# Additive attention: half of the softmax exponentials as powers of e on GpSimd, in eight pieces each

## The chip, the cores and the metric

The kernel runs on one core of a Trainium2 chip. The metric is device time in microseconds (us) of one execution; lower is better. A core has five engines, each with a queue of its own that it works off strictly in order: PE (TensorE, matrix products), DVE (VectorE), ACT (ScalarE, table functions such as tanh and exp), POOL (GpSimd) and SP (SyncE, which issues transfers). Engines wait for one another through semaphores, so an instruction that waits holds up everything behind it in its own queue.

## The reference, cut to what matters

The network has four layers over x of shape (2, 256, 32, 32). The change lies in the attention of the last layer, which runs over B = 2 images of L = 1024 tokens with D = 256 channels and U = 32 hidden units:

```python
q = jnp.einsum('bld,du->blu', inputs, Wt)
k = jnp.einsum('bld,du->blu', inputs, Wx)
h = jnp.tanh(q[:, :, None, :] + k[:, None, :, :] + bh)
e = jnp.einsum('biju,u->bij', h, Wa[:, 0]) + ba[0]
a = jax.nn.softmax(e, axis=-1)
v = jnp.einsum('bij,bjd->bid', a, inputs)
```

In front of it in the program stands a mixture of experts (top 2 of 8, with gelu), behind it another one. For every pair of tokens there are 32 tanh, 67 million in all, and one exponential, 2 million in all.

## The kernel before, in words

**Tiles and groups.** The 2048 queries are cut into NT = 16 tiles of 128, eight for each image. A tile is worked in M = 8 groups, 128 groups in all; a group is a tile `th` of 128 x 4 x 1024 elements (4 queries x 32 units on the partitions, 4 sets of queries, 1024 keys). For group n:

- `add(n)` (L1336): four DVE instructions of 128x1024 add the query to all keys and write `th`, which has three buffers.
- `tangents(n)` (L1346): one ACT instruction of 128x4096 takes tanh in place. For the 34 "light" groups in the middle (n from 50 to 83) ACT adds one of the four sets itself (L1343, L1344), and DVE has three.
- `score(n)` (L1355): sixteen PE matmul passes sum over the units with the weights Wa into the PSUM tile `ps_e`, 128x1024, of which there is one buffer; eight groups fill it.

**Softmax and values of tile i**, in group n = 8(i+1), when its eight groups are scored: `additive_softmax` (L1408) takes exp of `ps_e` on ACT into `p`, summing each row on the way; L1409 takes the reciprocal of the sum on DVE. Two groups later `turn` transposes the first half of `p` on PE and DVE copies it out (L1368, L1369), one group later the second half, and one more group later `values` multiplies with the tokens (L1376, L1380), and `done` takes the statistics of the finished tile for the next norm.

**Order of the work.** One Python loop runs over n and calls, for each n, `add(n + 2)`, `tangents(n)`, the softmax of the tile that has just ended, `score(n)`, then turns or values; so adds are issued two groups ahead of the tanh. Around each n the caller also steps other work on the same engines: up to n = 61 the rest of the experts before (`second`, one step every two groups) and the projections for the second image (`then`), afterwards the routing of the last layer and its first experts (`first`, one step every four groups). An expert's step has products on PE (L1175, L1189, L1205), their copies on DVE (L1163, L1183, L1211), gelu on ACT (L1192), weights fetched by SP, and two indirect transfers issued by POOL (L1146 gathers the tokens of a block, L1212 scatters its results). A scheduler of the framework decides at build time how the instructions of these strands stand in each engine's queue; in the running kernel the queues are fixed.

**Tables.** ACT's functions come from sets of tables; the instruction ACT_TABLE_LOAD changes the set. In the profile it stands before an exp that follows a gelu (L1408) and before a gelu that follows an exp (L1192); tanh never has one before it.

Of the kernel before, what the change touches and what calls it, by code (L numbers as in the profile page):

```python
# [8 lines left out]

# [1 line left out]

# [11 lines left out]
F32 = mybir.dt.float32  # L25
# [3 lines left out]
AF = mybir.ActivationFunctionType  # L29
ALU = mybir.AluOpType  # L30
AX = mybir.AxisListType
PSUM = bass.MemoryType.PSUM

P = 128
B, C, N = 2, 256, 1024
T = B * N
NT = T // P
CC = C // P
CH = 512
# [48 lines left out]
class Stack:  # L88
# [757 lines left out]
    def tables(self):  # L846

        nc = self.nc
        tl = lambda name, shape, dtype=F32: self.const.tile(shape, dtype, name=f"dp_{name}")
        ctx = ExitStack()  # L850
        tmp = ctx.enter_context(self.tc.tile_pool(name="dp_tmp", bufs=1))
        iota = lambda t, pattern, base, by: nc.gpsimd.iota(
            t, pattern=pattern, base=base, channel_multiplier=by, allow_small_or_imprecise_dtypes=True
        )
        self.iota_lo = tl("lo", [P, P], BF16)
        iota(self.iota_lo, [[1, P]], 0, 0)
        self.iota_hi = tl("hi", [P, BOTH], BF16)
        iota(self.iota_hi, [[1, BOTH]], 0, 0)
        self.iota_block = tl("block", [1, BOTH])
        iota(self.iota_block, [[1, BOTH]], 0, 0)  # L860
        self.partition = tl("partition", [P, 1])
        iota(self.partition, [[0, 1]], 0, 1)


        self.spare = tl("spare", [P, BOTH])
        iota(self.spare, [[P, BOTH]], P + 2 * T, 1)
        self.number = tl("number", [P, B, 2, N // P], BF16)
        iota(self.number, [[2 * N // P, B], [N // P, 2], [1, N // P]], 1, 0)

        before = tmp.tile([P, P], F32, name="dp_before")  # L870
        nc.gpsimd.memset(before, 1.0)
        nc.gpsimd.affine_select(
            before, before, pattern=[[1, P]], compare_op=ALU.is_gt, fill=0.0, base=0, channel_multiplier=-1
        )
        self.before = tl("before_bf", [P, P], BF16)
        nc.vector.tensor_copy(self.before, before)

        W = N // P * E
        d = tmp.tile([W, W + E], I32, name="dp_d")
        iota(d, [[1, W + E]], 0, -1)  # L880
        low = tmp.tile([W, W + E], I32, name="dp_low")
        nc.vector.tensor_scalar(low, d, E - 1, None, ALU.bitwise_and)
        same = tmp.tile([W, W + E], F32, name="dp_same")
        nc.vector.tensor_scalar(same, low, 0.0, None, ALU.is_equal)
        later = tmp.tile([W, W + E], F32, name="dp_later")
        nc.vector.tensor_scalar(later, d, 0.0, None, ALU.is_gt)
        self.earlier = tl("earlier", [W, W + E], BF16)
        nc.vector.tensor_tensor(self.earlier, same, later, ALU.mult)
        self.ones_bf = tl("ones", [P, P], BF16)
        nc.vector.memset(self.ones_bf, 1.0)  # L890
        ctx.close()
# [425 lines left out]
    def additive_attention(self, ctx, aa, t, u, light, done):  # L1317


        tc, nc = self.tc, self.nc  # L1320
        U, R, J, M = self.UNITS, self.ROWS, self.GROUPS, self.FOURS
        sb = ctx.enter_context(tc.tile_pool(name="aa_sb", bufs=1))
        p_e, p_t = (ctx.enter_context(tc.tile_pool(name=f"aa_{n}", bufs=1, space=PSUM)) for n in "et")
        groups = [(i, m) for i in range(NT) for m in range(M)]
        summed, scored = {}, {}

        def keys_and_queries(n, j):
            i, m = groups[n]
            b = i // (N // P)
            return aa["kT"][:, b * N : (b + 1) * N], aa["qb"][:, i, j * M + m : j * M + m + 1]  # L1330

        def add(n):

            h = sb.tile([P, J, N], F32, name="th", bufs=3)
            for j in range(1 if light(n) else 0, J):
                nc.vector.tensor_scalar(h[:, j, :], *keys_and_queries(n, j), None, ALU.add)  # L1336
            summed[n] = h

        def tangents(n):
            h = summed[n]  # L1340
            if light(n):
                keys, query = keys_and_queries(n, 0)
                nc.scalar.activation(h[:, 0, :], keys, AF.Tanh, bias=query)  # L1343
                nc.scalar.activation(h[:, 1:, :], h[:, 1:, :], AF.Tanh)  # L1344
            else:
                nc.scalar.activation(h, h, AF.Tanh)  # L1346

        def score(n):
            i, m = groups[n]
            if m == 0:  # L1350
                scored[i] = p_e.tile([P, 2, CH], F32, name="ps_e")
            h = summed.pop(n)
            for a in range(2):
                for j in range(J):
                    nc.tensor.matmul(  # L1355
                        scored[i][U * j : U * (j + 1), a, :], lhsT=aa["pick"][:, m, :],
                        rhs=h[:, j, a * CH : (a + 1) * CH], start=(m == 0), stop=(m == M - 1),
                    )

        turned = {}  # L1360

        def turn(i, p, a):

            if a == 0:
                turned[i] = sb.tile([P, N // P, P], F32, name="ptT")
            pt = p_t.tile([P, 4, P], F32, name="ps_pt")
            for j in range(4):
                nc.tensor.transpose(pt[:, j, :], p[:, (4 * a + j) * P : (4 * a + j + 1) * P], self.ident)  # L1368
            nc.vector.tensor_copy(turned[i][:, 4 * a : 4 * a + 4, :], pt)  # L1369

        def values(i, rec):
            b = i // (N // P)
            ptT = turned.pop(i)
            av = p_t.tile([P, 4, P], F32, name="ps_pt").rearrange("p k q -> p (k q)")[:, 0:C]
            for j in range(N // P):
                nc.tensor.matmul(  # L1376
                    av, lhsT=ptT[:, j, :], rhs=u[:, b * (N // P) + j, :],
                    start=(j == 0), stop=(j == N // P - 1),
                )
            nc.vector.scalar_tensor_tensor(t[:, i, :], av, rec, t[:, i, :], ALU.mult, ALU.add)  # L1380


        soft = {}
        add(0)
        add(1)
        for n in range(len(groups) + 5):
            if n + 2 < len(groups):
                add(n + 2)
            if n < len(groups):
                tangents(n)  # L1390
            i, m = n // M - 1, n % M
            if i >= 0 and m == 0:
                soft[i] = self.additive_softmax(aa, sb, scored.pop(i))
            if n < len(groups):
                score(n)
            if i >= 0 and m in (2, 3):
                turn(i, soft[i][0], m - 2)
            if i >= 0 and m == 4:
                values(i, soft.pop(i)[1])
                done(i)  # L1400
            yield n

    def additive_softmax(self, aa, sb, pe):

        nc = self.nc
        s, rec = (self.small.tile([P, 1], F32, name=f"aa_{n}") for n in ("s", "rec"))
        p = sb.tile([P, N], F32, name="p")
        nc.scalar.activation(p, pe.rearrange("p a b -> p (a b)"), AF.Exp, bias=aa["ba"], accum_out=s)  # L1408
        nc.vector.reciprocal(rec, s)  # L1409
        return p, rec  # L1410

# [287 lines left out]
class General(Stack):  # L1699
# [446 lines left out]
                    scores(i + 1)  # L2146
                values(i)

    def additive_softmax(self, aa, sb, pe):
        nc = self.nc  # L2150
        m, nb, s, rec = (self.small.tile([P, 1], F32, name=f"aa_{n}") for n in ("m", "nb", "s", "rec"))
        nc.vector.tensor_reduce(m, pe, AX.XY, ALU.max)

        nc.vector.tensor_tensor(m, m, aa["ba"], ALU.add)
        nc.vector.scalar_tensor_tensor(nb, m, -1.0, aa["ba"], ALU.mult, ALU.add)
        p = sb.tile([P, N], F32, name="p")
        nc.scalar.activation(p, pe.rearrange("p a b -> p (a b)"), AF.Exp, bias=nb, accum_out=s)
        nc.vector.reciprocal(rec, s)
        return p, rec
# [98 lines left out]
```

## Time and profile before

| | us |
|---|---|
| median of three runs | 2495.07 (2486.7 to 2497.26) |
| the profiled execution | 2487.81 |
| its span in the profile | 2486.0 |
| additive attention, by the tanh in it | about 1737 to 2295 |
| ACT busy between 1740 and 1950, of 210.00 | 202.53 |
| ACT busy between 1950 and 2100, of 150.00 | 141.11 |
| ACT busy between 2100 and 2300, of 200.00 | 183.94 |
| DVE busy in the same three stretches | 168.94, 118.54, 153.40 |
| POOL busy in the same three stretches | 20.05, 7.06, 28.51 |

The profile is of one execution. Its time is 1.8 us above its span, and 7.3 us under the median. "Busy" is the time in which an engine works on an instruction; of PE it overstates, since matmuls are pipelined. A group's row gives line, engine, operation, output and inputs with shapes, the number of instructions, the busy time, the mean of one in ns, and the idle time before them with what ended it. A timeline's row gives the start, the duration, and in brackets the idle time of the engine before it with its cause.

### The profile page before, as it was taken

The page shows a single profiled execution, that of the slowest core. Times are in us where ns is not written, and L with a number is a line of the kernel's source. Part 1 is how long each engine was busy: PE and PEld are TensorE (multiplying, and loading weights), DVE is VectorE, ACT ScalarE, POOL GpSimd, SP SyncE. Part 2 cuts the span into 40 slices and gives each one's busy share as a digit, 9 for nine tenths or more (in the row PEclk, how much of TensorE's full clock was granted, in tenths as well). Part 3 has the DMA queues.
Part 4 walks back from the last instruction along what each step waited for, and adds up shares of the span by engine and source line. Part 5 has one row for each costly group of instructions (what it writes and reads, how often), then busy time and mean ns, then how long its engine had stood idle before and what let it go on. Part 6 is the DMA issues. An engine that isn't in the chain of part 4 may idle for free.

```text
span 2486.0 us, 42312 instructions
## 1 busy us (share of the span) xinstructions
PE 2337.5 (94%) x17179; PEld 1017.8 (41%) x17179; DVE 1710.7 (69%) x2656; ACT 1398.4 (56%) x1445; POOL 238.4 (10%) x253
## 2 busy tenths in 40 slices
PE   7999999999999999999998969998999888988987
PEld 4333333333333333333333646665444433333654
DVE  5677777785677777876679566226887778876533
ACT  1565556555555556554444333221999999998122
POOL 0000000000000000000002212221110001111332
PEclk9999999999999999999999979999999999999998
DMA  4000000000000000000000036777444103323986
GB/s 140 1 1 1 1 1 1 1 5 1 1 1 1 1 1 1 6 1 1 1 1 10 2 120 252 291 291 269 185 157 187 60 9 104 107 89 110 335 324 232
DMA packets 65121, 205.46 MB, mean 83 GB/s; under 512 B 15060, under 2 KB 29908, under 8 KB 54932
## 3 DMA queue, kind: packets, MB, share of 16 engines
q1 hardware_dynamic: 51428, 176.81, 19.7%
q0 software_dynamic: 8160, 22.29, 2.5%
q10 hardware_dynamic: 5328, 3.55, 0.5%
q8 instruction: 137, 2.24, 0.4%
q14 instruction: 68, 0.56, 0.1%
HBM read 183.09 MB, written 17.44 MB: 81 GB/s over the span
## 4 chain that ended last, share of the span: by engine, by line
PE 72%; DVE 13%; issue 6%; DMA 5%; ACT 3%; POOL 1%; SPq 0%; ACTq 0%; DVEq 0%; POOLq 0%
PE ps_o L237 20%; PE ps_t L215 20%; PE ps_e L1355 7%; PE bk_y L1205 4%; PE bk_h L1175 4%; DVE th L1336 4%; DMA w<-in_l_w 3%; PE ps_row L460 2%; DVE sum L227 2%; PE ps_pt L1376 2%; PE ps_qk L569 1%; PE ps_row L450 1%; PE ps_row L489 1%; PE bk_t L1189 1%; DVE den L263 1%
## 5 line engine op out<-in xcount | busy, mean ns | idle before, releaser
L218 ACT ACTIVATE e<-ps_t 128x1024 f32<-128x1024 f32 x640 | 652.2, 1023 | 481.8 <-PE ps_t L216 470.6
L227 DVE TENSOR_TENSOR sum<-sum,e 128x1024 f32<-128x1024 f32 x592 | 726.2, 1227 | 280.2 <-ACT e L218 268.8
L237 PE MATMUL ps_o<-e,v 64*64 64x512 f32 x5120 | 663.4, 590 | 11.0 <-DVE o L244 7.2
L215 PE MATMUL ps_t<-q,k 64*64 64x512 f32 x2048 | 528.0, 590 | 0.5 <-DVE v L610 0.5
L216 PE MATMUL ps_t<-q,k 64*64 64x512 f32 x2048 | 527.9, 590 | 0.0
L1336 DVE TENSOR_SCALAR th<-kT,qb 128x1024 f32<-128x1024 f32 x478 | 330.6, 750 | 88.0 <-PE ps_e L1355 85.7
L1346 ACT ACTIVATE th<-th 128x4096 f32<-128x4096 f32 x94 | 335.7, 3616 | 16.8 <-DVE th L1336 16.5
L237 PEld LDWEIGHTS ps_o<-e,v 64*64 64x64 f32 x5120 | 191.1, 131 | 371.2 <-issue 178.6
L1355 PE MATMUL ps_e<-th,pick 128*32 128x512 f32 x2048 | 264.3, 613 | 17.7 <-ACT p L1408 9.4
L215 PEld LDWEIGHTS ps_t<-q,k 64*64 64x64 f32 x2048 | 148.0, 133 | 287.4 <-issue 153.0
L1175 PE MATMUL bk_h<-w,xgT 128*128 128x512 f32 x496 | 244.3, 610 | 13.6 <-DVE xgT L1163 7.4
L1205 PE MATMUL bk_y<-w,h 128*128 128x256 f32 x992 | 246.5, 385 | 5.9 <-DVE y L1211 3.2
L1205 PEld LDWEIGHTS bk_y<-w,h 128*128 128x128 f32 x992 | 178.7, 191 | 49.0 <-issue 21.3
L1197 ACT ACTIVATE h<-bk_t,w 128x128 f32<-128x128 f32 x276 | 78.7, 368 | 211.9 <-issue 115.8
L265 POOL TENSOR_TENSOR inverses<-inverses,den 128x512 f32<-128x512 f32 x24 | 30.4, 1268 | 1319.3 <-DVE den L263 1319.3
L216 PEld LDWEIGHTS ps_t<-q,k 64*64 64x64 f32 x2048 | 148.0, 133 | 0.0
L1175 PEld LDWEIGHTS bk_h<-w,xgT 128*128 128x128 f32 x496 | 87.1, 194 | 93.9 <-issue 66.4
L1212 POOL DMA_INDIRECT given<-y,gives x85 | 85.9, 1011 | 400.3 <-DVE y L1211 337.2
L1355 PEld LDWEIGHTS ps_e<-th,pick 128*32 128x32 f32 x2048 | 58.1, 111 | 160.1 <-issue 124.4
L1181 DVE COPY hp<-bk_h 128x512 f32<-128x512 f32 x69 | 47.6, 691 | 106.1 <-PE bk_h L1175 106.1
L1146 POOL DMA_INDIRECT xg<-rows,takes x85 | 86.5, 1017 | 325.6 <-PE bk_x L1158 275.2
L215 PE MATMUL ps_t<-qh,kh 64*64 64x512 f32 x384 | 98.7, 598 | 0.0
(344 smaller groups left out, 2194.3 us busy)
## 6 DMA issues: line engine op xcount, KB each, us to landing
w<-in_l_w SPq DMA_DIRECT2D x39, 1152.0 KB, 5.4
w<-in_l_w SPq DMA_DIRECT2D x39, 1030.0 KB, 7.3
w<-in_l_w SPq DMA_DIRECT2D x46, 640.0 KB, 6.8
w<-in_l_w SPq DMA_DIRECT2D x46, 514.0 KB, 5.8
b<-in_l_w SPq DMA_DIRECT2D x16, 512.0 KB, 8.3
b<-in_l_w SPq DMA_DIRECT2D x23, 256.0 KB, 5.4
rows<-u SPq DMA_DIRECT2D x8, 512.0 KB, 2.9
uT<-given SPq DMA_DIRECT2D x32, 128.0 KB, 3.2
```

Source lines behind the costliest of these rows:

```text
L215: nc.tensor.matmul(ps[part, 0, :], lhsT=ka[:, part], rhs=q[0:64, :], start=True, stop=True)
L216: nc.tensor.matmul(ps[part, 1, :], lhsT=kb[:, part], rhs=q[64:128, :], start=True, stop=True)
L218: nc.scalar.activation(e, ps, AF.Exp)
L227: nc.vector.tensor_tensor(c["sum"], c["sum"], e, ALU.add)
L237: nc.tensor.matmul(c["po"][64 * r : 64 * r + 64, half, :], lhsT=v[part, :], rhs=e[part, r, :], start=(j == 0), stop=(j == c["n"] - 1),)
L1146: nc.gpsimd.indirect_dma_start(out=tokens[b], out_offset=None, in_=rows(b)[:, :], in_offset=index(slots(b)[0], b))
L1175: nc.tensor.matmul(ps, lhsT=inputs[b][:, c, :], rhs=first[b][:, at : at + CH], start=(c == 0), stop=(c == CC - 1),)
L1205: nc.tensor.matmul(sums[b], lhsT=h[:, j * P : (j + 1) * P], rhs=second[b][:, at : at + C], start=(n == 0 and j == 0), stop=(n == HH - 1 an ...
L1212: nc.gpsimd.indirect_dma_start(out=given[b], out_offset=index(slots(b)[1], b), in_=y, in_offset=None)
L1336: nc.vector.tensor_scalar(h[:, j, :], *keys_and_queries(n, j), None, ALU.add)
L1346: nc.scalar.activation(h, h, AF.Tanh)
L1355: nc.tensor.matmul(scored[i][U * j : U * (j + 1), a, :], lhsT=aa["pick"][:, m, :], rhs=h[:, j, a * CH : (a + 1) * CH], start=(m == 0), sto ...
```

## The change

For the even tiles (0, 2, ..., 14) the exponential is no longer taken by ACT. DVE copies `ps_e` into `p` in two halves and adds the bias `ba`; POOL then raises e to each element in place, in eight instructions of 128x128, with a column of e's read with a stride of zero; DVE sums the rows with one reduction, and takes the reciprocal as before. The turns of such a tile come five and seven groups after the softmax and its values eight groups after, where they came two, three and four groups after. `p` gets two buffers. The odd tiles are computed and placed as before. (The other class in the file, which runs only if a range check fails, is not changed in what it does.)

```diff
+        self.euler = tl("euler", [P, 1])
+        nc.vector.memset(self.euler, math.e)
...
+        for i in range(NT):
+            at = (i + 1) * M
+            due.setdefault(at, []).insert(0, lambda i=i: softmax(i))
+            for n, f in zip((5, 7, 8) if self.powers(i) else (2, 3, 4), (
+                lambda i=i: turn(i, soft[i][0], 0), lambda i=i: turn(i, soft[i][0], 1), lambda i=i: finish(i)
+            )):
+                later(at + n, f)
...
-            i, m = n // M - 1, n % M
-            if i >= 0 and m == 0:
-                soft[i] = self.additive_softmax(aa, sb, scored.pop(i))
+            todo = due.pop(n, [])
+            if n % M == 0 and todo:
+                todo.pop(0)()
             if n < len(groups):
                 score(n)
-            if i >= 0 and m in (2, 3):
-                turn(i, soft[i][0], m - 2)
-            if i >= 0 and m == 4:
-                values(i, soft.pop(i)[1])
-                done(i)
+            for f in todo:
+                f()
             yield n
 
-    def additive_softmax(self, aa, sb, pe):
+    def powers(self, i):
+        return i % 2 == 0
+
+    def additive_softmax(self, aa, sb, pe, i):
         nc = self.nc
         s, rec = (self.small.tile([P, 1], F32, name=f"aa_{n}") for n in ("s", "rec"))
-        p = sb.tile([P, N], F32, name="p")
-        nc.scalar.activation(p, pe.rearrange("p a b -> p (a b)"), AF.Exp, bias=aa["ba"], accum_out=s)
+        p = sb.tile([P, N], F32, name="p", bufs=2)
+        if self.powers(i):
+            for a in range(2):
+                nc.vector.tensor_scalar(p[:, a * CH : (a + 1) * CH], pe[:, a, :], aa["ba"], None, ALU.add)
+            for j in range(N // P):
+                x = p[:, j * P : (j + 1) * P]
+                nc.gpsimd.tensor_tensor(x, self.euler.to_broadcast([P, P]), x, ALU.pow)
+            nc.vector.tensor_reduce(s, p, AX.X, ALU.add)
+        else:
+            nc.scalar.activation(p, pe.rearrange("p a b -> p (a b)"), AF.Exp, bias=aa["ba"], accum_out=s)
         nc.vector.reciprocal(rec, s)
         return p, rec
```

More of the change, by code (lines that the diff above doesn't have):

```diff
@@ L12 @@
+import math
 from contextlib import ExitStack
@@ L1380, in values, with softmax, finish @@
             nc.vector.scalar_tensor_tensor(t[:, i, :], av, rec, t[:, i, :], ALU.mult, ALU.add)
-        soft = {}
+        soft, due = {}, {}
+        later = lambda n, f: due.setdefault(n, []).append(f)
+        def softmax(i):
+            soft[i] = self.additive_softmax(aa, sb, scored.pop(i), i)
+        def finish(i):
+            values(i, soft.pop(i)[1])
+            done(i)
+        for i in range(NT):
[5 more added lines that the diff above has]
+                later(at + n, f)
         add(0)
@@ L2147, in window_attention, with powers, additive_softmax @@
                 values(i)
-    def additive_softmax(self, aa, sb, pe):
+    def powers(self, i):
+        return False
+    def additive_softmax(self, aa, sb, pe, i):
         nc = self.nc
```

## The prediction

> **What bounds the kernel now.** I read the busy slices of the page first, for the place: the stretch in which ACT shows 9 is the additive attention.
>
> ```profile
> DVE  5677777785677777876679566226887778876533
> ACT  1565556555555556554444333221999999998122
> POOL 0000000000000000000002212221110001111332
> ```
>
> A slice is 62 us; from about 1737 to 2295 us ACT is the fullest engine, and POOL is nearly empty. Next the costliest groups and the groups by line, shapes kept apart, to see what fills ACT and what the engines that get the work charge for the like:
>
> ```profile
> L1346 ACT ACTIVATE th<-th 128x4096 f32<-128x4096 f32 x94 | 335.7, 3616 | 16.8 <-DVE th L1336 16.5
> L1408 ACT ACTIVATE p<-ps_e,sb_ba 128x1024 f32<-128x1024 f32 x16 | 17.8, 1112 | 5.3 <-PE ps_e L1355 5.2
> L1408 ACT ACT_TABLE_LOAD x12 | 15.4, 1283 | 0.2
> L1192 ACT ACT_TABLE_LOAD x13 | 16.7, 1283 | 2.1 <-PE bk_t L1189 1.9
> L265 POOL TENSOR_TENSOR inverses<-inverses,den 128x512 f32<-128x512 f32 x24 | 30.4, 1268 | 1319.3 <-DVE den L263 1319.3
> L686 POOL TENSOR_TENSOR t<-t,sb_wa_b_out 128x256 f32<-128x256 f32 x16 | 11.2, 737 | 2.2 <-DVE u L160 1.3 <-DVE sb_wa_b_out L684 0.9
> L1369 DVE COPY ptT<-ps_pt 128x512 f32<-128x512 f32 x32 | 21.9, 686 | 0.4 <-PE ps_pt L1368 0.4
> L841 DVE TENSOR_REDUCE extremes<-every 128x1 f32<-128x4097 f32 x1 | 4.4, 4411 | 0.0
> ```
>
> The tanh waits little (16.8 us over 94 instructions), so here a microsecond off ACT is nearly a microsecond off the span, as long as DVE delivers the adds in time. How much time DVE has to spare decides the case, so the last view is the timeline of ACT and of DVE around the softmax of tile 0 (n = 8).
>
> ```profile
> 1762.86 7.13 ACT L1346 ACTIVATE th<-th 128x4096 f32<-128x4096 f32 x2
> 1770.01 1.28 ACT L1408 ACT_TABLE_LOAD   x1
> 1771.31 1.11 ACT L1408 ACTIVATE p<-ps_e,sb_ba 128x1024 f32<-128x1024 f32 x1
> 1772.32 0.19 ACT L1408 ACTIVATION_READ_ACCUMULATOR p<-ps_e,sb_ba 128x1 f32 x1
> 1772.53 1.28 ACT L1192 ACT_TABLE_LOAD   x1
> 1773.82 0.60 ACT L1192 ACTIVATE h<-bk_t 128x512 f32<-128x512 f32 x1
> 1774.32 7.12 ACT L1346 ACTIVATE th<-th 128x4096 f32<-128x4096 f32 x2
> ```
>
> ```profile
> 1770.24 2.73 DVE L1336 TENSOR_SCALAR th<-kT,qb 128x1024 f32<-128x1024 f32 x4
> 1772.89 0.42 DVE L1211 TENSOR_TENSOR y<-bk_y,w 128x256 f32<-128x256 f32 x1
> 1773.23 0.69 DVE L1183 TENSOR_TENSOR hp<-bk_h,b 128x512 f32<-128x512 f32 x1
> 1773.84 0.15 DVE L1409 RECIPROCAL aa_rec<-aa_s 128x1 f32<-128x1 f32 x1
> 1776.20 2.74 DVE L1336 TENSOR_SCALAR th<-kT,qb 128x1024 f32<-128x1024 f32 x4 [2.20 <-PE ps_e L1355]
> ```
>
> The first ACT row holds tanh 7 and 8, the last one 9 and 10. The adds at 1770.24 are those of group 10, those at 1776.20 of group 11, ready at 1778.9; tanh 11 starts at 1781.8. DVE is therefore 2.9 us early, not several groups.
>
> **Taken from ACT.** One exp with its sum takes 1772.53 - 1771.31 = 1.22 us; eight go: 9.8 us. Without the exp between them, tanh and gelu need no change of tables: in the changed program's ACT queue 7 loads stand before an exp instead of 12, and 5 fewer before a gelu. Ten loads at 1.29 us (1770.01 to 1771.31 with the gap) are 12.9 us. Together 22.7 us, all in the stretch where ACT is the bound. The rows show the exp 0.02 us after the end of the load, and the load 0.02 us after tanh. The Trainium skill ("ScalarE: Activation LUTs", What ACT_TABLE_LOAD costs) adds some 1.38 us of drain to each switch; by that the ten would bring 26.6 us and the sum below would be 13.7 us lower, but no such gap is in this trace.
>
> **Given to DVE.** For an even tile two copies from PSUM with the bias, 128x512 each, by L1369 0.69 us: 1.4 us. One reduction of 1024 columns: L841 takes 4411 ns for 4097, a quarter with some start is 1.2 us. Eight times 2.6 us is 21 us; DVE has about a fifth of this stretch idle, so as load they would hide. As waits they don't, and this is the step that decides.
>
> **The wait that is added.** In the changed program's DVE queue, tile 0 reads: adds of group 10, the two copies of p, y and hp of an expert, the reduction, one more hp, the reciprocal, and only then the adds of group 11. The other even tiles have the same order: the reduction ahead of the adds of group n + 3. The reduction waits for all eight powers, so every add behind it does too, and ACT has no more than the tanh of n + 1 and n + 2 to work on. The later turns and values relieve PE, not this. Call X the time from the first power to the last. Tile 0: adds of group 10 end at 1772.9 as before, copies at 1774.3, powers at 1774.3 + X, reduction 1.2, hp and reciprocal 0.85, adds 2.65: tanh 11 can start at 1779.0 + X. Without the exp and its loads ACT would be there at 1769.99 + 0.6 + 7.1 + 0.5 = 1778.1. The stall is X + 0.9. The same working at tile 4 (tanh n ends at 1915.2 there, and its last adds at 1915.0) gives X - 1.0, and at tile 12 (tanh at 2187.9) X - 2.4, because DVE is further ahead there. I take the mean, X - 0.8, for all eight: **the change is worth 8 (X - 0.8) - 22.7 us**, and breaks even at X = 3.6 us, or 0.45 us a power.
>
> **What a power costs.** No row shows one. POOL's two shapes of TENSOR_TENSOR give (1268 - 737) / 256 = 2.07 ns a column and 207 ns of start: one pass over 128 columns is 0.27 us, an add of 128x128 0.47 us. That is the lower end: X = 3.8, sum +1 us. A still lower one would be POOL's memset of 128x128 at 0.20 us (L100, 202 ns): X = 1.6, sum -16 us. A power can't be one pass of arithmetic. The kernel's own inverse square root (L131 to L138) takes 4 + 9 = 13 elementwise steps; thirteen passes of 0.27 us with one start are 3.7 us, X = 29.3, sum +205 us. A logarithm and an exponential of that length each, 26 passes, are 7.1 us, X = 57, sum +427 us. Steps inside one instruction need no trip to memory, so I put a power at half of the thirteen, about 2.0 us: X = 16, and the sum is 8 x 15.2 - 22.7 = **+99 us**. This is an estimate between far ends, and most of the range comes from it. The Trainium skill ("GPSIMD Engine Reference", 2.1 Instruction dispatch) speaks of about 6 us without a visible instruction at the first call of freshly loaded code on GpSimd; no row here shows it, and by it the sum would be 6 us higher, once.
>
> **What else moves.** POOL's queue: the gathers (L1146) and scatters (L1212) of experts stand behind eight powers in a row. They are issued some three blocks ahead of their use, a block being four groups or some 15 us, so up to X = 30 nothing waits for them; beyond that they add to a stall that is already counted. PE: score(n) waits for the copies of p (1774.3) where it started at 1774.20; nothing. The transposes of p stand behind score(n + 3), which needs the adds behind the reduction: the powers are over by then. The values of the last even tile come in group 128, four before the last tile's, which is computed as before: the end of the stage doesn't move by it. The second buffer of p costs no time.
>
> **Rivals.** (1) As forecast, a power between 0.8 and 3.7 us: +22 to +205 us. Chance 0.61. (2) The power is worked element by element or in long chains, over 3.7 us: +205 to +427 us, and POOL becomes the bound of these groups. For it: thirteen or more steps by the kernel's own row. Against: POOL's adds run at 2 ns a column, no sign of a loop per element. Chance 0.20. (3) The power costs about what an add costs, 0.47 to 0.8 us: +1 to +22 us, saving and stall nearly cancel. Chance 0.13. (4) Faster: the reduction is released before DVE could have started the next adds anyhow. The place is the DVE queue between the reduction and the adds of n + 3, the price is the whole of ACT's saving less the rest of the stall, -16 us at 0.20 us a power, and it decides from 0.45 us down. For it: DVE's own wait for score(8) there, 2.20 us in the row above. Against: every arithmetic row of POOL is dearer. Chance 0.06. That the exponentials don't leave ACT is ruled out by its queue.
>
> **How the numbers follow.** The profiled execution took 2487.8 us, so by its own rows 2587; the median of the runs lies 7.3 us above it, and I forecast on the median: 2495.1 + 99 = 2594 us. The range leaves out (4), most of (3) and the upper part of (2): from +10 us (X = 4.9) to +265 us (X = 36.8), 2505 to 2760 us. About 0.5%, 12.5 us, is what a measurement of this kernel can tell from no change. Faster by that: nearly all of (4), 0.05. Within: the rest of (4) and the part of (3) below +12.5 us, 0.08. Slower: 0.87.
>
> **What would show it.** Right: eight times in the stretch DVE idle for about X in front of the reduction, released by POOL, and right behind it ACT idle in front of tanh for nearly as long, by L1336; POOL rows of 128x128 at about 2 us; 7 loads before exp; the additive stretch longer by about 100 us and everything outside it unchanged. The step on X is wrong if those POOL rows differ from 2 us, the step on the slack if ACT's wait is far from X - 0.8 at a tile. The forecast falls if DVE's wait for POOL is under 3.6 us a tile, or if ACT doesn't wait behind it.

## The result, and the profile after

The changed kernel takes 3799.24 us (median of 4 runs, 3794.62 to 3807.62); the kernel before took 2491.40 us beside it. The ratio is 1.5249, with a 95% interval of 1.5216 to 1.5281: slower by about half. The forecast was slower, but by 99 us, and the range ended at 2760 us. The profiled execution took 3794.62 us, 1306.8 us more than the one before.

The busy slices show where the time went. A slice is 95 us now.

```profile
DVE  5777775777776876436041050410504114050253
ACT  2555655555554433224042060510604105060222
POOL 0000000000000031223958939489394895949732
PEclk9999999999999998998576585755857657585699
```

From the 20th of the 40 slices to the 38th, ACT shows 0 wherever POOL shows 9, and DVE shows 0 or 1 there. Up to 1740 us the two profiles agree in every engine's busy time within 2 us. The last tanh ends 196.9 us before the end of the span in the kernel before (2289.1 of 2486.0) and 194.5 us before it now. So the whole change lies inside the additive attention. The lines of the costliest groups say what fills it:

```profile
L1436 POOL TENSOR_TENSOR p<-dp_euler,p 128x128 f32<-128x128 f32 x64 | 1324.4, 20713 | 114.8 <-DVE p L1433 114.7
L1437 DVE TENSOR_REDUCE aa_s<-p 128x1 f32<-128x1024 f32 x8 | 9.8, 1220 | 1067.4 <-POOL p L1436 1067.4
L1349 ACT ACTIVATE th<-th 128x4096 f32<-128x4096 f32 x94 | 335.6, 3613 | 1015.7 <-DVE th L1339 1015.5
L1371 PE MATMUL ps_pt<-ident,p 128*128 128x128 f32 x128 | 32.8, 343 | 752.4 <-POOL p L1436 668.1
L1439 ACT ACT_TABLE_LOAD x7 | 9.0, 1283 | 0.1
L1195 ACT ACT_TABLE_LOAD x8 | 10.3, 1283 | 1.8 <-PE bk_t L1192 1.7
```

Read them from the top: a power of 128x128 takes 20.71 us, where the forecast had 2.0. The reduction waits for POOL, and the tanh waits for DVE's adds: the chain of waits that the prediction described. Neither of these two rows holds the whole wait, since the powers take 1324.4 us; what else waits is shown below. The work of ACT itself is as forecast: 7 loads before an exp instead of 12, and 8 instead of 13 before a gelu. The timeline around the first even tile (start, duration, in brackets the idle time before and its cause; POOL, then DVE, then ACT) shows the same chain once:

```profile
1774.60 165.57 POOL L1436 TENSOR_TENSOR p<-dp_euler,p 128x128 f32<-128x128 f32 x8
```

```profile
1772.38 1.40 DVE L1433 TENSOR_SCALAR p<-ps_e,sb_ba 128x512 f32<-128x512 f32 x2
1773.70 0.41 DVE L1214 TENSOR_TENSOR y<-bk_y,w 128x256 f32<-128x256 f32 x1
1774.03 0.68 DVE L1186 TENSOR_TENSOR hp<-bk_h,b 128x512 f32<-128x512 f32 x1
1940.21 1.22 DVE L1437 TENSOR_REDUCE aa_s<-p 128x1 f32<-128x1024 f32 x1 [165.50 <-POOL p L1436]
1941.35 0.68 DVE L1186 TENSOR_TENSOR hp<-bk_h,b 128x512 f32<-128x512 f32 x1
1941.94 0.15 DVE L1440 RECIPROCAL aa_rec<-aa_s 128x1 f32<-128x1 f32 x1
1942.01 8.03 DVE L1339 TENSOR_SCALAR th<-kT,qb 128x1024 f32<-128x1024 f32 x12
```

```profile
1776.10 0.58 ACT L1195 ACTIVATE h<-bk_t 128x512 f32<-128x512 f32 x1
1944.85 7.13 ACT L1349 ACTIVATE th<-th 128x4096 f32<-128x4096 f32 x2 [168.18 <-DVE th L1339]
```

Here DVE's queue is in the forecast order: copies, y, hp, reduction, hp, reciprocal, adds. At tiles 8, 12 and 14 it is not: there DVE stands first at the copy of the transposed first half of `p`, for some 82.6 us, and at the reduction only for the other half of the powers. Tile 8:

```profile
2800.27 0.69 DVE L1372 COPY ptT<-ps_pt 128x512 f32<-128x512 f32 x1 [82.82 <-PE ps_pt L1371]
2882.48 1.22 DVE L1437 TENSOR_REDUCE aa_s<-p 128x1 f32<-128x1024 f32 x1 [81.51 <-POOL p L1436]
```

Three such copies are the 248 us that the reduction's row lacks of the eight waits. ACT waits as long at every even tile, but at tile 6 in two pieces (42.37 us for PE's scores, 122.62 us for DVE's adds) and at tile 8 in front of the routing's exponential (L940, 163.00 us for DVE), so the tanh of L1349 shows only six of the eight waits. PE's 668.1 us at the transposes (L1371) are waits for the powers too, most of them at tiles 6 to 14.

At the first even tile almost nothing else happens on the core between 1780 and 1940 us; PE's 20 matmuls take 3.57 us (the columns are the window, its length, then busy time and instructions of PE, PEld, DVE, ACT and POOL, the granted clock, DMA share and GB/s):

```profile
1780.00:1940.00 160.00, 3.57 (x20) 2.59 (x16) 0.00 (x0) 0.00 (x0) 160.00 (x8) 0.52 0.02 7
```

### The profile page after: what moved, and what is told of

Read it like the earlier page. It is cut to its first block, busy times and chain, and to the rows that moved or that the text cites. A ratio compares the mean times of both kernels' runs of the same rounds, so it can differ in the third digit from the quotient of the medians.

```text
span 3792.8 us, 42396 instructions
## 1 busy us (share of the span) xinstructions
PE 2374.1 (63%) x17179; PEld 1028.6 (27%) x17179; DVE 1730.0 (46%) x2681; ACT 1376.6 (36%) x1419; POOL 1564.0 (41%) x317
## 3 DMA queue, kind: packets, MB, share of 16 engines
q1 hardware_dynamic: 51428, 176.81, 12.9%
## 4 chain that ended last, share of the span: by engine, by line
PE 44%; POOL 33%; DVE 9%; issue 8%; DMA 3%; ACT 3%; SPq 0%; ACTq 0%; DVEq 0%; POOLq 0%
POOL p L1436 32%; PE ps_o L238 13%; PE ps_t L216 13%; PE ps_e L1358 3%; PE bk_h L1178 3%; PE bk_y L1208 2%; DVE th L1339 2%; PE ps_row L461 1%; DVE sum L228 1%; PE ps_pt L1379 1%; DMA w<-in_l_w 1%; ACT th L1349 1%; PE ps_qk L570 1%; PE ps_row L451 1%; DVE den L264 1%
## 5 line engine op out<-in xcount | busy, mean ns | idle before, releaser
L1436 POOL TENSOR_TENSOR p<-dp_euler,p 128x128 f32<-128x128 f32 x64 | 1324.4, 20713 | 114.8 <-DVE p L1433 114.7
L1349 ACT ACTIVATE th<-th 128x4096 f32<-128x4096 f32 x94 | 335.6, 3613 | 1015.7 <-DVE th L1339 1015.5
L1371 PE MATMUL ps_pt<-ident,p 128*128 128x128 f32 x128 | 32.8, 343 | 752.4 <-POOL p L1436 668.1
L1437 DVE TENSOR_REDUCE aa_s<-p 128x1 f32<-128x1024 f32 x8 | 9.8, 1220 | 1067.4 <-POOL p L1436 1067.4
L1358 PE MATMUL ps_e<-th,pick 128*32 128x512 f32 x2048 | 281.0, 655 | 271.9 <-ACT th L1349 174.9
L1192 PE MATMUL bk_t<-ident,hp 128*128 128x128 f32 x496 | 80.0, 281 | 279.4 <-DVE aa_rec L1440 274.5
L1371 PEld LDWEIGHTS ps_pt<-ident,p 128*128 128x128 f32 x128 | 16.9, 155 | 787.1 <-POOL p L1436 682.3
L216 PEld LDWEIGHTS ps_t<-q,k 64*64 64x64 f32 x2048 | 148.2, 133 | 288.2 <-issue 153.1
L1149 POOL DMA_INDIRECT xg<-rows,takes x85 | 86.2, 1015 | 303.4 <-PE bk_x L1161 253.4
```

The source lines that it names most:

```text
L216: nc.tensor.matmul(ps[part, 0, :], lhsT=ka[:, part], rhs=q[0:64, :], start=True, stop=True)
L1358: nc.tensor.matmul(scored[i][U * j : U * (j + 1), a, :], lhsT=aa["pick"][:, m, :], rhs=h[:, j, a * CH : (a + 1) * CH], start=(m == 0), sto ...
L1436: nc.gpsimd.tensor_tensor(x, self.euler.to_broadcast([P, P]), x, ALU.pow)
```

## The experiments

Nine kernels, two of them measured twice, in three groups that share their runs of the kernel before. Theory A is in most of them the prediction's mechanism with the measured price: what is lost is the time that DVE's queue stands at the sum of the powers. In experiments 3 and 4 it is a theory of what a power costs.

**1. Is it the power, or the form?** The same instructions in the same places, with `add` in place of `pow`:

```diff
-                nc.gpsimd.tensor_tensor(x, self.euler.to_broadcast([P, P]), x, ALU.pow)
+                nc.gpsimd.tensor_tensor(x, self.euler.to_broadcast([P, P]), x, ALU.add)
```

> The eight instructions per even tile are adds instead of powers, with the same operands, order and waits; the weights are then wrong by that. Theory A (the price lies in the power function itself, and the stall is 8 (X - 0.8) - 22.7 us as worked out): POOL rows of 128x128 at about 0.47 us, X about 3.8 us, the time within 0.5% of before, 2485 to 2500 us. Theory B (the price lies in the form, a column read with stride zero, in place, in small pieces): rows still at about 20 us, the time near 3790 us. Theory C (GpSimd working beside VectorE slows both, whatever it does): rows well above 0.47 us and the time above 2530 us.

Measured: 2491.98 us against 2489.73, ratio 1.0010 [0.9998, 1.0023]. The 1300 us are gone; the kernel is within some 6 us of the one before. Its POOL group:

```profile
L1436 POOL TENSOR_TENSOR p<-dp_euler,p 128x128 f32<-128x128 f32 x64 | 23.5, 401 | 114.7 <-DVE p L1433 114.7
```

An add takes 0.40 us, so the column of e's, the shape and the number of instructions are not what costs. This run also stands for rival (3), a power as dear as an add: the forecast had it at +1 us with 0.47 us each. That nothing is won has its place in ACT's waits for DVE's adds between 1737 and 2300 us: the two forms of the tanh wait 43.8 us, where they waited 18.0 (16.5 and 1.5) before. The 25.8 us more take back the 22.7 us that ACT saves.

```profile
ACT th L1349 <- DVE th L1339: 39.2, 17, 5.5
ACT th L1347 <- DVE th L1339: 4.6, 5, 1.3
```

**2. What is there to be gained at most?** No work on GpSimd at all: the even tiles get ones in place of exponentials, written by the two DVE copies; sum, turns and values stay where the change puts them.

```diff
-                nc.vector.tensor_scalar(p[:, a * CH : (a + 1) * CH], pe[:, a, :], aa["ba"], None, ALU.add)
-            for j in range(N // P):
-                x = p[:, j * P : (j + 1) * P]
-                nc.gpsimd.tensor_tensor(x, self.euler.to_broadcast([P, P]), x, ALU.pow)
+                nc.vector.tensor_scalar(p[:, a * CH : (a + 1) * CH], pe[:, a, :], 0.0, 1.0, ALU.mult, ALU.add)
```

> No GpSimd instruction at all for the even tiles: VectorE writes ones in its two copies and sums them, so their weights are uniform; all else as in the change. It shows what ACT's relief is worth once no power stands in the way. Theory A: X = 0, the saving of 22.7 us less what stays of the stall: 2465 to 2478 us. Rival: the adds bind as soon as ACT is relieved and nothing comes of it: 2485 to 2495 us.

Measured: 2475.58 us, ratio 0.9941 [0.9924, 0.9959]. If GpSimd's part were free, the change would bring 0.6%. Measured again, beside two kernels of experiment 7:

> The kernel with neither powers nor exponentials in the even tiles again, to be compared with the two that follow on the same chip: 12 to 17 us faster than before.

2476.12 us against 2493.24, ratio 0.9937 [0.9924, 0.9951].

**3. What sets the price of a power?** Each even tile of one kernel does the powers in its own way: pieces of 64, 128, 256 or 1024 columns, 8 or 64 partitions in place of 128, base 1, exponent 1, and adds in tile 12.

```diff
+            elif i == 2:
+                nc.gpsimd.tensor_tensor(p, e.to_broadcast([P, N]), p, ALU.pow)
+            elif i == 4:
+                for j in range(16):
+                    x = p[:, j * 64 : (j + 1) * 64]
+                    nc.gpsimd.tensor_tensor(x, e.to_broadcast([P, 64]), x, ALU.pow)
+            elif i == 6:
...
+                    x = p[0:8, j * P : (j + 1) * P]
+                    nc.gpsimd.tensor_tensor(x, e[0:8].to_broadcast([8, P]), x, ALU.pow)
...
```

> The powers of each even tile in another form: tile 0 eight of 128x128; tile 2 one of 128x1024; tile 4 sixteen of 128x64; tile 6 eight of 8x128 and eight of 64x128, on ones; tile 8 base 1; tile 10 exponent 1; tile 12 adds; tile 14 four of 128x256 (weights wrong in tiles 6 to 12). Theory A (each element costs its own time, partitions one after the other within a GpSimd core, cores side by side): 165.7, 10.4 and 41.4 us for 1024, 64 and 256 columns; 64 partitions as dear as 128 (20.7 us), 8 partitions half of that; base or exponent 1 perhaps cheaper. Rival D (a fixed price of an instruction): one of 1024 far below 165 us and 64 columns near 20 us. Rival E (lanes in step): 8 partitions as dear as 128.

Measured, in POOL's groups (the second number after the bar is the mean of one instruction in ns):

```profile
L1444 POOL TENSOR_TENSOR p<-dp_euler,p 128x64 f32<-128x64 f32 x16 | 167.8, 10509 | 11.5 <-DVE p L1433 11.5
L1438 POOL TENSOR_TENSOR p<-dp_euler,p 128x128 f32<-128x128 f32 x8 | 165.6, 20740 | 0.0
L1440 POOL TENSOR_TENSOR p<-dp_euler,p 128x1024 f32<-128x1024 f32 x1 | 163.3, 163252 | 2.6 <-DVE p L1433 2.6
L1449 POOL TENSOR_TENSOR p<-dp_euler,p 8x128 f32<-8x128 f32 x8 | 165.7, 20724 | 21.4 <-DVE p L1446 21.4
L1456 POOL TENSOR_TENSOR p<-ones,p 128x128 f32<-128x128 f32 x8 | 166.0, 20776 | 70.0 <-DVE p L1433 70.0
L1460 POOL TENSOR_TENSOR p<-dp_euler,ones 128x128 f32<-128x128 f32 x8 | 165.6, 20713 | 0.7 <-DVE p L1433 0.7
L1464 POOL TENSOR_TENSOR p<-dp_euler,p 128x128 f32<-128x128 f32 x8 | 2.9, 392 | 0.6 <-DVE p L1433 0.6
```

(163252 - 20740) / 896 columns is 159 ns a column, with some 0.4 us of start, against 2.07 ns a column that the prediction took for an add: 77 times as much. Beyond that start, neither the size of a piece, nor the height of the tile (8 or 128 partitions), nor the values (1 to any exponent, e to the exponent 1) move it. Cutting the tile into eight pieces therefore changes next to nothing in its price. Eight partitions cost what 128 cost, so the price goes by columns and not by elements: rival E held, and Theory A, which had half the price for eight partitions, fell on this point. How the engine shares the partitions of a column out, the runs don't tell. The kernel took 3796.33 us in its one run.

**4. Is it only this operation?** Again one kernel with another operation in each tile: subtraction, multiplication, the power on bf16, the power with a constant exponent, an add of two full operands.

```diff
+            if i == 0:
+                for x in parts:
+                    nc.gpsimd.tensor_tensor(x, e, x, ALU.subtract)
+            elif i == 2:
+                for x in parts:
+                    nc.gpsimd.tensor_tensor(x, e, x, ALU.mult)
...
+            elif i == 8:
+                for x in parts:
+                    nc.gpsimd.tensor_tensor(x, e, self.two.to_broadcast([P, P]), ALU.pow)
...
```

> Other operations in the place of the powers: in tile 0 a subtraction, in tile 2 a multiplication, in tile 6 the power on bf16 (copied there and back by VectorE), in tile 8 the power of e with the constant exponent 2 read with a stride of zero, in tile 10 an add with full operands on both sides; tiles 4, 12 and 14 keep the exponential on ScalarE. Theory A (the power alone is dear, and every element costs the same, whatever it is): subtraction and multiplication 0.40 us each, the power on bf16 and with a constant exponent 20.7 us each; the add of two full operands 0.47 us, as the rows of 128x256 and 128x512 gave. Rival: the dearness is that of every operation but the add (the multiplication over 1 us), or the power on bf16 is worked at half the price.

Measured:

```profile
L1440 POOL TENSOR_TENSOR p<-dp_euler,p 128x128 f32<-128x128 f32 x8 | 2.9, 393 | 0.0
L1443 POOL TENSOR_TENSOR p<-dp_euler,p 128x128 f32<-128x128 f32 x8 | 2.9, 393 | 1.9 <-DVE p L1435 1.9
L1449 POOL TENSOR_TENSOR low<-dp_euler,low 128x128 bf16<-128x128 f32 x8 | 165.7, 20735 | 22.6 <-DVE low L1446 22.6
L1453 POOL TENSOR_TENSOR p<-dp_euler,dp_two 128x128 f32<-128x128 f32 x8 | 165.5, 20715 | 71.2 <-DVE p L1435 71.2
L1456 POOL TENSOR_TENSOR p<-ones,p 128x128 f32<-128x128 f32 x8 | 3.4, 453 | 0.6 <-DVE p L1435 0.6
```

As Theory A had it: subtraction (L1440) and multiplication (L1443) cost what the add costs, and the power costs 20.7 us with exponent and result in bf16 (the f32 of its row is the base, which stays f32) and with a constant exponent as well. An operand that is one column read with a stride of zero saves 0.06 us against two full ones (L1456). The kernel's time, 2831.94 us, is about that of two tiles of powers; it decides nothing.

**5. Does each tile pay by itself?** Powers in tile 0 alone:

```diff
     def powers(self, i):
-        return i % 2 == 0
+        return i == 0
```

> Powers for tile 0 alone, the other fifteen tiles on ACT with the old places. Theory A (each tile pays for itself: X - 0.8 less a saving of 2.8 us): 164.8 - 2.8 = 162 us more than before, 2645 to 2660 us, everything after the stall as before. Rival G (the stalls of the change feed on one another, by the lower clock of TensorE and the work that piles up): clearly less than an eighth of the 1307 us, under 150 us.

Measured: 2654.53 us against 2492.49, 162.0 us more. The sum for one tile, X - 0.8 less an eighth of the saving, is 165.6 - 0.8 - 2.8 = 162.0; one run can't be trusted to more than some 5 us, so that the two agree to the decimal is chance, and the wait itself is X + 1.8, not X - 0.8. But seven eighths of the loss are gone with seven eighths of the powers. ACT waits once:

```profile
1948.24 3.62 ACT L1349 ACTIVATE th<-th 128x4096 f32<-128x4096 f32 x1 [167.40 <-DVE th L1339]
```

**6. Is it the place of the sum in DVE's queue?** The sum and the reciprocal move from the softmax to the values, eight groups later, so that no add stands behind them:

```diff
-            values(i, soft.pop(i)[1])
+            p, rec, s = soft.pop(i)
+            if self.powers(i):
+                nc.vector.tensor_reduce(s, p, AX.X, ALU.add)
+                nc.vector.reciprocal(rec, s)
+            values(i, rec)
```

> The sum and the reciprocal of an even tile stand where its values are, eight groups after the softmax, so VectorE no longer waits for POOL ahead of the adds of group n + 3. Theory A: the wait only moves: the transposes five groups on stand in PE's queue ahead of the scores and need the powers too, so each tile gains no more than the two or three groups in between, about 8 to 20 us: 3640 to 3730 us. Rival F (the sum's wait is the fault, POOL could work beside the rest): below 3300 us, down to POOL's own 8 x 165.7 = 1326 us in place of the stage's 558, about 3260 us.

Measured: 3674.41 us in one run, 120 us less than the changed kernel's own profiled execution; the powers are as dear as before. The waits (who waits for whom: total us, number, longest) show where the rest went:

```profile
PE ps_pt L1371 <- POOL p L1440: 1159.3, 61, 26.6
DVE ptT L1372 <- PE ps_pt L1371: 889.4, 14, 82.8
```

PE's queue stands at the transposes, one power at a time, for 1159.3 us in place of 668.1, and DVE's queue at the copies of what they deliver, for 889.4 in place of 248.7. Theory A's range (3640 to 3730 us) held. With 165 us of powers for every second tile and some 70 us that two tiles took before (16 tiles in 552 us), POOL itself can't keep up: eight tiles of powers are 1325 us whatever waits for them. The rival that expected less than 3300 us fell.

**7. Is the same true at the price of an add?** Experiments 1 and 6 together: adds in place of powers, and the late sum.

> Adds in place of powers (weights wrong by that), and the sum and reciprocal of the even tiles eight groups later, beside the values. The kernel with adds and the early sum took as long as before, the one without GpSimd work 14 us less. Theory A: what those adds still cost is VectorE's wait for them and the sum in front of the adds of group n + 3, which is gone here: 2470 to 2480 us. Rival H (the cost is GpSimd working beside VectorE, or the wait for TensorE instead): 2485 to 2495 us.

Measured: 2485.14 us against 2492.49, ratio 0.9972 [0.9958, 0.9986]: faster than before, by 7 us, where 12 to 22 were expected. That is the edge of rival H's range (2485 to 2495 us). No wait of DVE for POOL is left, yet half of what experiment 2 showed is missing. Two more kernels, run beside experiment 2's, asked whether that was chance, and whether GpSimd's adds slow VectorE down. The first repeats the last kernel; the second is experiment 2's with the 64 adds put back, writing to a scratch tile that nobody reads:

```diff
+            scratch = sb.tile([P, P], F32, name="scratch")
+            for j in range(N // P):
+                part = slice(j * P, (j + 1) * P)
+                nc.gpsimd.tensor_tensor(scratch, self.euler.to_broadcast([P, P]), p[:, part], ALU.add)
```

> The kernel with adds instead of powers and the late sum again. If the difference of some 7 us to the kernel with neither was chance, the two agree here within 3 us; if it is real, they are 5 to 9 us apart again.

> The kernel with neither, plus the same 64 GpSimd adds written to a scratch tile for which nobody waits. Theory A (an add on GpSimd costs only what waits for it): the same time as without them, within 3 us. Rival H (the GpSimd adds slow VectorE while they run): 5 us or more slower than without, with the VectorE adds beside them longer than elsewhere (above 750 ns).

Measured: 2484.36 us (0.9960 [0.9947, 0.9974]) for the repeat, 2474.56 us (0.9923 [0.9910, 0.9937]) with the idle adds, 2476.12 us for neither. The idle adds of GpSimd cost the kernel nothing that shows. They do slow VectorE, and VectorE them, but only while both run: where tile 0's adds meet VectorE's adds for the tanh (window 1778.3 to 1782.1 us), VectorE's take 885 ns and GpSimd's 734, against 748 in the kernel with neither and 399 as the median of the idle adds.

```profile
L1339 DVE TENSOR_SCALAR th<-kT,qb 128x1024 f32<-128x1024 f32 x5 | 4.1, 885 | 0.0
L1437 POOL TENSOR_TENSOR scratch<-dp_euler,p 128x128 f32<-128x128 f32 x5 | 3.7, 734 | 0.3
```

Some fifteen of the 478 adds for the tanh meet them so, about 2 us in all, and the mean of all 478 rises only from 748 to 752 ns. In the repeat, GpSimd's adds take 406 ns on average, so they hardly meet VectorE's there. The 8 us between the repeat and the kernel with neither are real, and not contention. The last exponential comes 8.3 us later in the repeat (2292.96 against 2284.67), and 6.3 of these arise between the exponentials of tiles 7 and 9, which are 72.6 us apart in place of 66.3. The windows of 1950 to 2100 us (columns as above; first the kernel with neither, then the repeat) cover that place: ACT does 9 us less work in it.

```profile
1950.00:2100.00 150.00, 126.27 (x770) 50.20 (x768) 123.68 (x321) 138.17 (x85) 4.48 (x5) 0.94 0.16 53
```

```profile
1950.00:2100.00 150.00, 124.41 (x742) 49.63 (x744) 120.15 (x308) 129.10 (x81) 8.59 (x19) 0.93 0.13 44
```

What in the order of that stretch costs them (the late sum, or the turns that now wait for POOL) stays open.

**8. Can the table loads be saved without GpSimd?** DVE copies both tiles of a pair out of PSUM, and ACT takes the two exponentials one after the other, once for two tiles, with the turns later:

```diff
+            if self.powers(i):
+                self.held = p, s, rec
+                return p, rec
+            q, sq, rq = self.held
...
+            nc.scalar.activation(q, q, AF.Exp, bias=zero, accum_out=sq)
+            nc.scalar.activation(p, p, AF.Exp, bias=zero, accum_out=s)
```

> No GpSimd: VectorE copies the scores of both tiles of a pair out of PSUM, and ACT takes the two exponentials one after the other when the second tile is scored, so that a pair needs one change of tables and back instead of two (ten loads fewer, as in the change); the turns of the even tile come ten groups after its scores, of the odd one four. ACT gets 12.9 us less, VectorE 22 us more. Theory A (both count in this stretch, ACT the more): 2 to 10 us faster, 2480 to 2488 us. Rival: VectorE's added copies stand in front of the adds and take it all back: 2488 to 2500 us.

Measured: 2493.97 us against 2492.49, ratio 1.0012 [1.0000, 1.0023]. No gain: the range of the rival (2488 to 2500 us) held. DVE got 32 copies where the kernel before has none, and the tanh now waits 22.0 us for adds where it waited 16.5. That is not the whole of the 12.9 us that ACT saves; its gelu (L1195) also waits 9.3 us for PE in this stretch where it waited 2.9, and which copy causes which wait was not followed up.

```profile
L1436 DVE TENSOR_SCALAR p<-ps_e,sb_ba 128x512 f32<-128x512 f32 x32 | 22.6, 741 | 3.7 <-PE ps_e L1358 3.7
L1349 ACT ACTIVATE th<-th 128x4096 f32<-128x4096 f32 x93 | 331.6, 3614 | 22.1 <-DVE th L1339 22.0
```

No kernel that takes all the exponentials beat the one before.

## Why the prediction failed, step by step

**The step that failed is the price of a power.** The prediction said: "Steps inside one instruction need no trip to memory, so I put a power at half of the thirteen, about 2.0 us". Measured: 20.71 us, ten times that. Put into the prediction's own sum, with X = 165.6 us for the eight, the rest of it gives 2487.8 + 8 x 164.8 - 22.7 = 3783.5 us for the profiled execution, which took 3794.6. So one term carries the miss. It rested on "steps inside one instruction", half of thirteen; no run shows such a step, and the experiments show in its place a price of 159 ns for every column. That everything behind the sum waits for the powers held; two details of the queues did not, and the slack was mis-sized (below).

**Its two bounds were not bounds.** Thirteen and 26 passes are counts of another algorithm on another engine, priced by GpSimd's add. That the add runs at 2.07 ns a column was taken as "no sign of a loop per element", against rival (2). It is a fact about adds: experiments 3 and 4 show 159 ns a column for the power beside three operations at the price of an add, on the same engine in the same form. The upper end, 7.1 us, is a third of what was measured. Rival (2), with its "long chains" and POOL as the bound, was the right direction at too small a size: the measured loss lies beyond every rival's prices. The trace of before held no row from which 20 us could be read; it held none either that excluded it, and the range should have been open above. The Trainium skill ("GPSIMD Engine Reference", 2.1 Instruction dispatch) was weighed for some 6 us at the first call; the first eight powers take 165.57 us and the mean eight 165.55 (1324.4 / 8), and the first of them begins 0.02 us after the gather in front of it, so no such cost shows here.

**The saving on ACT held.** Five loads fewer before exp and five before gelu, 1.28 us each and a gap of 0.01 to 0.02, and eight exps: 22.7 us as forecast, by ACT's rows. No drain beyond the load shows, as before.

**DVE's queue held in what decides.** At every even tile DVE stands until the last power, the adds behind the reduction wait with it, and ACT starves for as long. The order fits five of the eight tiles. The prediction had the transposes "behind score(n + 3)", with the powers "over by then"; in fact PE stood at them for 668.1 us, and at tiles 8, 12 and 14 the copy of their first half stands ahead of the reduction in DVE's queue. This changed no time here, because the wait ends at the last power either way; but it goes with experiment 6, where moving the sum alone gained 120 us of 1307. Experiment 1 takes the price away and the loss goes with it; experiment 5 shows the price of one tile; experiment 6 moves the sum, and most of the wait moves to the transposes.

**The slack was mis-sized by 1.1 us a tile.** ACT's waits at the eight even tiles are 168.2, 167.3, 167.2, 165.0, 163.0, 164.6, 165.7 and 166.2 us: on average X + 0.3, where the prediction took X - 0.8. At the three tiles that it had worked out, 0, 4 and 12, the forecast was X + 0.9, X - 1.0 and X - 2.4, and found were X + 2.6, X + 1.7 and X + 0.1. (For tile 0 the terms shown add up to X + 0.8; 1778.1 should be 1778.2.) Tile 0 shows how. ACT stood 1.7 us further on than in the trace of before (tanh 8 ended at 1768.3, not at 1770.0) and was through at 1776.7 instead of 1778.1, while POOL's first power began 0.3 us later than forecast, behind a gather (L1149, 0.96 us, from 1773.62). Eight times 1.1 is 8.7 us of the 11 that the sum leaves over; the other 2 are less than the runs of one kernel differ. With that slack the break-even is X = 2.5 us, 0.32 us a power, in place of 0.45; an add at X = 2.9 comes to +3 us, and experiment 1 measured +2. So close a fit is partly luck: at X = 0 the same sum gives -20 us, and experiment 2 measured -14 and -17.

**POOL's other work.** The prediction let its gathers and scatters wait for nothing up to X = 30. X is far beyond that, but the eight stalls sum to 1327 us, which is 8 X and some 3 us: those transfers are late inside the stall and add nothing that shows.

## What to carry to other kernels

The price of one operation on an engine need not say anything of another operation on the same engine, even in the same form: here they differ 50 times. Where the deciding term has no row, leave the range open on that side, or measure one instruction of it before anything is moved. Do not take the mean of a whole group for the time of the few instructions that are in question: GpSimd's effect on VectorE is hidden in such a mean, and plain in a narrow window. Ask as well what the move is worth if it were free: here 0.6% against a loss of half. And look in the queue of the engine that collects the result for the work that stands behind the collecting instruction, since a wait there is paid by whoever needs that work.

## What the runs showed of the hardware

A power on GpSimd takes 159 ns a column, for 8 partitions as for 128, with exponents and results in f32 and in bf16, for every pair of operands tried, while add, subtract and multiply of 128x128 take 0.39 to 0.40 us. GpSimd's adds and VectorE's adds of 128x1024 slowed one another while both ran (0.73 in place of 0.40 us, and 885 in place of 748 ns, in the window of experiment 7). Its powers did not slow them: in experiment 6, 16 of VectorE's adds between 1780 and 1818 us, while two powers run, take 750 ns on average, and the powers 20.75 us. TensorE's granted clock fell where the engine had next to nothing to do: 0.52 in the window of the first wait above, and 0.816 over the whole execution against 0.982 before. The first score after that wait takes 3.43 us, the next one 1.92:

```profile
1948.53 3.43 PE L1358 MATMUL ps_e<-th,pick 128*32 128x512 f32 x16 [164.95 <-ACT th L1349]
...
1953.38 1.92 PE L1358 MATMUL ps_e<-th,pick 128*32 128x512 f32 x16
```

That was not in the prediction. PE is not what ACT waits for there, and whether some of the last 2 us are owed to it was not tried.
